# Last layer of a four-layer graph network: whole tiles for four of its elementwise steps, transposes in pairs of banks, and a fixed order on every engine

## The chip, the cores and the metric

One core of a Trainium2 chip. A core has five engines with queues of their own: TensorE (PE, with its weight loads shown apart as PEld), VectorE (DVE), ScalarE (ACT), GpSimd (POOL) and SyncE (SP, which here only issues DMAs). They share the on-chip memory SBUF; PE writes its results to PSUM, eight banks of 512 f32 columns in each of the 128 partitions. An engine works through its queue in order and stops at an instruction whose inputs are not there yet. The metric is the device time of one execution in microseconds.

## What is computed

`reference(x, adj, ...)` runs four graph layers over 4096 nodes with 64 features, each followed by a residual and a layer norm: a Chebyshev polynomial, a gated attention, a decayed neighbour sum, and a hyperbolic layer. Only the last one is touched by the change:

```python
deg = jnp.maximum(adj.sum(axis=1, keepdims=True), 1e-08)
w = adj / deg
log_ij = _logmap(x[:, None, :], x[None, :, :], c)     # for every pair of nodes
agg = jnp.einsum('ij,ijc->ic', w, log_ij)
transformed = agg @ weight + bias
return _expmap(origin, transformed, c)
```

`_logmap` needs, for each pair (i, j), one inner product, and from it a number: `arctanh(n) / n` of a norm. The kernel computes this factor for each pair, multiplies `adj` by it, and multiplies the result by the matrix of node vectors.

## The kernel before

**Tiles.** The 4096 x 4096 matrix is cut into 8 x 8 tiles of 512 x 512, held as 128 partitions x 4 blocks x 512 columns (2048 columns). The factor is symmetric, so only the 36 tiles on and above the diagonal are worked on: `tiles` (L1469) lists them by rows, 8 tiles in the first row (the diagonal one first), then 7, 6, ... 1; the groups come in the order `seq`. Of a diagonal tile only the upper part is computed: its first half has 512 columns in each of two blocks, its second half 256. The other 28 tiles are used twice: the tile of A itself (`own`, at_d) is multiplied by the factor, and the tile on the other side of the diagonal (`mirrored`, at_m) by the transposed factor.

**Halves.** The loop (L1719) counts half tiles: n = 2t + h, two blocks, 1024 columns each (512 for the second half of a diagonal tile). For each half the steps are, with engine and line:

1. `product` (PE, L1507): inner products into `v_ps`, two PSUM banks, two such buffers.
2. `square` (ACT, L1516): w = v squared. Then `opposite` (PE, L1526) adds a second product to `v_ps`.
3. `less_one` (DVE, L1534): w less one, with a floor.
4. Ln (ACT, L1731), then rt = Exp(0.5 Ln w), the root (ACT, L1732), and w = Exp(-0.5 Ln w), the reciprocal root (ACT, L1758).
5. rt = max(v, ..) + rt (DVE, L1756); after it `v_ps` is free for the product two halves later.
6. rt = Ln(rt), the last logarithm (ACT, L1767).
7. f = min(rt, ..) x w, the factor (DVE, L1741), and own x f (DVE, L1744), two halves behind step 4.
8. `turn` (PE, L1552): four transposes of 128 x 128 into one bank "post", four times for an off-diagonal tile; after each bank one product with `mirrored` (DVE, L1554). A diagonal tile has one bank (L1545) and one such product (L1547).
9. `gather` (PE, L1568, L1580): per block, the node vectors times the own product into the lower half of a row's bank `sums_ps`, and times the mirrored product of the tile before into the upper half. The first of the upper ones is a matmul that carries in the sum so far (L1576); at the end ACT copies the upper half out (L1587). At the end of a row the lower half is copied out as well (L1591).

**What else runs there.** `seam` is a list of steps of which one is taken in each half: at first the last steps of the layer before (`ends`, L1273: norms and preparation, L1286 to L1228), then, for each finished row, `finals` (L1644): `first` (16 matmuls L1660, three DVE steps, four L1670 on ACT), `second`, `third`, `fourth`, `fifth` (layer norm and store). `right(i)` (L1456) prepares the right side for a new row: 12 matmuls (L1461) into two "post" banks and two copies on ACT (L1464).

**Order.** The program is handed to a scheduler, which puts each engine's instructions into an order by their place in the program and by its own estimate of when their inputs are there. Only some PE instructions (product, opposite, gather) are tied to program order by `in_order` (L205). DMAs of tiles are issued on SP, three buffers each for own and mirrored.

**PSUM.** Eight banks: `ps_v3` 2 x 2, `ps_a3` 2 (row sums), `ps_p3` 2 ("post", shared by transposes, right sides and seam).

Of the kernel before, what the change touches and what calls it, by code (L numbers as in the profile page):

```python
# [62 lines left out]
def gnn4_kernel(  # L63
# [144 lines left out]
    def cols(b):  # L208
        return slice(b * P, (b + 1) * P)
# [1229 lines left out]
    with tc.tile_pool(name="o3", bufs=1) as op, tc.tile_pool(name="cols3", bufs=3) as cols_p, tc.tile_pool(  # L1439
        name="w3", bufs=4  # L1440
    ) as wp3, tc.tile_pool(name="el3", bufs=3) as el, tc.tile_pool(name="f3", bufs=2) as fp, tc.tile_pool(
        name="r3", bufs=2
    ) as rp, tc.tile_pool(name="ps_v3", bufs=2, space=PSUM) as ps_v, tc.tile_pool(
        name="ps_a3", bufs=2, space=PSUM
    ) as ps_a, tc.tile_pool(name="ps_p3", bufs=2, space=PSUM) as ps_p:
        HB = CB // 2

# [40 lines left out]
        def columns(n):  # L1488

            i, j = tiles[n // 2]  # L1490
            return slice(2 * P if i == j and n % 2 else 0, GW)

        rights, sums, fs = {}, {}, {}
        vs, ws, rts = {}, {}, {}
        NU = 2 * NT

        def product(n):

            if n >= NU:
                return  # L1500
            i, j = tiles[n // 2]
            vs[n] = ps_v.tile([P, HB, GW], F32, name="v_ps")
            cs = columns(n)
            for k in range(HB):
                jb = j * CB + (n % 2) * HB + k
                half = slice(jb % 2 * F, jb % 2 * F + F)
                in_order(nc.tensor.matmul(  # L1507
                    vs[n][:, k, cs], lhsT=tr_c[half, jb // 2, :], rhs=rights[i][0][half, cs], start=True, stop=True
                ))

        def square(n):
            if n >= NU:
                return
            ws[n] = wp3.tile([P, HB, GW], F32, name="w3")
            cs = columns(n)
            nc.scalar.activation(ws[n][:, :, cs], vs[n][:, :, cs], AF.Square)  # L1516

        def opposite(n):
            if n >= NU:
                return  # L1520
            i, j = tiles[n // 2]
            cs = columns(n)
            for k in range(HB):
                jb = j * CB + (n % 2) * HB + k
                half = slice(jb % 2 * F, jb % 2 * F + F)
                in_order(nc.tensor.matmul(  # L1526
                    vs[n][:, k, cs], lhsT=tr_o[half, jb // 2, :], rhs=rights[i][1][half, cs],
                    start=False, stop=True, skip_group_check=True,
                ))

        def less_one(n):
            if n < NU:
                w = ws[n][:, :, columns(n)]
                nc.vector.tensor_scalar(w, w, -SCALE * SCALE, V_FLOOR * (V_FLOOR + 2.0) * SCALE**2, ALU.add, ALU.max)  # L1534

        def turn(n):

            t, h = n
            i, j = tiles[t]
            work = []  # L1540
            if i == j:
                tp = ps_p.tile([P, GW], F32, name="post", tag="post")
                for k in range(HB):
                    for b in range(HB):
                        nc.tensor.transpose(tp[:, cols(HB * k + b)], fs[t][:, b, cols(HB + k)], ident)  # L1545
                to = own[t][:, HB:CB, 0 : HB * P]
                work.append(lambda: nc.vector.tensor_tensor(to, tp.rearrange("p (k i) -> p k i", k=HB), to, ALU.mult))  # L1547
                return work
            for b in (HB * h, HB * h + 1):
                tp = ps_p.tile([P, GW], F32, name="post", tag="post")  # L1550
                for k in range(CB):
                    nc.tensor.transpose(tp[:, cols(k)], fs[t][:, k, cols(b)], ident)  # L1552
                to = mirrored[t][:, b, :]
                work.append(lambda to=to, tp=tp: nc.vector.tensor_tensor(to, tp, to, ALU.mult))  # L1554
            return work

        def gather(t, h, tm):

            if t is not None:
                i, j = tiles[t]  # L1560
                if i == j and h == 0:
                    sums[i] = ps_a.tile([P, GW], F32, name="sums_ps")
                bank = sums[i]
            else:
                bank = sums[seq[-1]]
            for k in (HB * h, HB * h + 1):
                if t is not None:
                    in_order(nc.tensor.matmul(  # L1568
                        bank[0:F, :], lhsT=nat_c[:, j * CB + k, :], rhs=own[t][:, k, :],
                        start=(i == j and k == 0), stop=(j == seq[-1] and k == CB - 1), skip_group_check=True,  # L1570
                    ))
                if tm is not None:
                    above, below = tiles[tm]
                    if k == 0 and above != seq[0]:

                        in_order(nc.tensor.matmul(  # L1576
                            bank[F:P, :], lhsT=ident[:, F:P], rhs=tb[:, gcols(below)],
                            start=True, stop=False, skip_group_check=True,
                        ))
                    in_order(nc.tensor.matmul(  # L1580
# [3 lines left out]
            work = []  # L1584
            if tm is not None and h:
                to = tb[F:P, gcols(tiles[tm][1])]
                work.append(lambda: nc.scalar.copy(to, bank[F:P, :]))  # L1587
            if t is not None and h and tiles[t][1] == seq[-1]:
                g = tiles[t][0]
                copy = nc.vector.tensor_copy if g == seq[-1] else nc.scalar.copy  # L1590
                work.append(lambda: copy(tb[0:F, gcols(g)], bank[0:F, :]))  # L1591
                seam.extend(finals(g))
            return work
# [113 lines left out]
        turns, late_turns, gathers = {}, {}, {}  # L1707

        for t in range(3):
            load_own(t)  # L1710
            load_mirrored(t)
        rights[seq[0]] = right(seq[0])
        product(0)
        square(0)
        less_one(0)
        opposite(0)
        product(1)
        n = 0
        while n < NU + 2 or turns or gathers:  # L1719
            if n % 2:  # L1720
                load_own((n + 1) // 2)
                load_mirrored((n - 1) // 2)
            after = gather(*gathers.pop(n)) if n in gathers else []
            turned = [w for what in turns.pop(n, []) for w in turn(what)]
            if n < NU:
                if n % 2 == 0:
                    fs[n // 2] = fp.tile([P, CB, GW], F32, name="f3")
                w, cs = ws[n][:, :, columns(n)], columns(n)
                rts[n] = el.tile([P, HB, GW], F32, name="rt3")
                rt = rts[n][:, :, cs]  # L1730
                nc.scalar.activation(w, w, AF.Ln)  # L1731
                nc.scalar.activation(rt, w, AF.Exp, scale=0.5)  # L1732
                square(n + 1)
                opposite(n + 1)
            if n >= 2 and n - 2 < NU:
                m = n - 2
                t, h = divmod(m, 2)
                cm = columns(m)
                hs = slice(h * HB, (h + 1) * HB)
                f, at = fs[t][:, hs, cm], own[t][:, hs, cm]  # L1740
                nc.vector.scalar_tensor_tensor(  # L1741
                    f, rts.pop(m)[:, :, cm], T_MAX, ws.pop(m)[:, :, cm], ALU.min, ALU.mult
                )
                nc.vector.tensor_tensor(at, at, f, ALU.mult)  # L1744
                diagonal = tiles[t][0] == tiles[t][1]
                before = t - 1 if t and tiles[t - 1][0] != tiles[t - 1][1] else None
                gathers[n + 1] = (t, h, before)
                if diagonal and h == 0:
                    late_turns[n + 1] = (t, 0)
                if not diagonal and h == 1:  # L1750
                    turns.setdefault(n + 1, []).append((t, 0))
                    turns.setdefault(n + 2, []).append((t, 1))
            for work in turned:
                work()
            if n < NU:
                nc.vector.scalar_tensor_tensor(rt, vs[n][:, :, cs], (1.0 + V_FLOOR) * SCALE, rt, ALU.max, ALU.add)  # L1756
                product(n + 2)
                nc.scalar.activation(w, w, AF.Exp, scale=-0.5)  # L1758
            late = turn(late_turns.pop(n)) if n in late_turns else []
            for work in after:  # L1760
                work()
            less_one(n + 1)
            for work in late:
                work()
            if 0 < n <= NU:
                rt = rts[n - 1][:, :, columns(n - 1)]
                nc.scalar.activation(rt, rt, AF.Ln, scale=1.0 / SCALE)  # L1767
            if n == NU - 6:
                seam += [ahead_of_last(g) for g in seq[-2:]]
# [58 lines left out]
```

## Time and profile before

| | us |
|---|---|
| median of 3 runs (1407.41 to 1412.98) | 1408.8 |
| the profiled execution: time | 1410.98 |
| the profiled execution: span | 1409.2 |
| busy in the span: PE / DVE / ACT | 1308.8 / 1051.4 / 805.0 |
| first square of the last layer (ACT L1516) starts | 972.07 |
| last gather matmul (PE L1580) ends | about 1387.95 |

The trace has one entry for every instruction: start and duration, engine, line, what it writes and reads with its shape, and in brackets how long its engine sat idle before it and what that wait ended on. Durations of DVE and ACT instructions overlap their successors a little, so the distance from one start to the next is what an instruction costs a full engine. Matmul ends are modelled. The page divides the span into 40 slices of 35.2 us; the last layer is slices 28 to 40.

### The profile page before, as it was taken

What the parts mean: (1) busy time and instruction counts of PE and PEld (TensorE: products, weight loads), DVE (VectorE), ACT (ScalarE), POOL (GpSimd) and SP (SyncE); (2) the same over time, 40 slices, a digit from 0 to 9 for tenths busy, and PEclk for the clock granted to TensorE, in tenths of its full rate; (3) what the DMA queues carried; (4) which work ended last, traced back from release to release, by engine and by line L of the source; (5) the groups of instructions that cost most, each with busy time, mean ns of one, the idle gap of its engine ahead of it and who ended that gap; (6) DMA issues with size and microseconds to landing.
All of it is one profiled execution on the core that took longest, in us unless ns stands there. A gap on an engine that the chain in (4) does not pass through costs nothing.

```text
span 1409.2 us, 18984 instructions
## 1 busy us (share of the span) xinstructions
PE 1308.8 (93%) x6766; PEld 605.2 (43%) x6766; DVE 1051.4 (75%) x2010; ACT 805.0 (57%) x1341; POOL 109.9 (8%) x191
## 2 busy tenths in 40 slices
PE   7999999999899999999999999997888898999883
PEld 5655555565344334444444323333333333333331
DVE  6699998999334257787885224356999999999996
ACT  4554444343000115654424675745989999999893
POOL 2111111101122000010111000000000000000000
PEclk9999999999999999999999999998999999999997
DMA  9999999999699999999985755534235353445320
GB/s 316 404 395 391 402 411 410 410 403 392 231 380 372 389 415 372 422 358 338 329 306 185 229 178 165 181 120 180 99 141 211 147 214 150 183 162 200 141 106 12
DMA packets 108191, 382.16 MB, mean 271 GB/s; under 512 B 20276, under 2 KB 20280, under 8 KB 76472
## 3 DMA queue, kind: packets, MB, share of 16 engines
q1 hardware_dynamic: 87096, 296.17, 56.8%
q0 software_dynamic: 12736, 76.29, 13.2%
q10 hardware_dynamic: 8256, 8.39, 1.7%
q8 instruction: 56, 0.92, 0.3%
q14 instruction: 47, 0.39, 0.1%
HBM read 294.05 MB, written 85.20 MB: 269 GB/s over the span
## 4 chain that ended last, share of the span: by engine, by line
PE 61%; ACT 15%; DVE 15%; DMA 5%; issue 3%; ACTq 0%; DVEq 0%; SPq 0%
PE pass L566 7%; PE tp L657 6%; PE w_ps L566 5%; DMA raw<-in_adj_dram 4%; PE cnt_ps L1380 4%; PE a_last L1111 4%; PE a_ps L1111 4%; PE pass L559 4%; PE acc_ps L1340 4%; PE h_ps L559 3%; PE wide_last L1102 2%; PE p_ps L1102 2%; DVE rt L1756 2%; ACT w L1731 2%; ACT rt L1732 2%
## 5 line engine op out<-in xcount | busy, mean ns | idle before, releaser
L664 ACT COPY at<-tp 128x512 f32<-128x512 f32 x248 | 127.9, 599 | 119.1 <-issue 95.9
L1385 ACT ACTIVATE wt<-cnt_ps 128x512 uint16<-128x512 f32 x210 | 116.5, 596 | 65.4 <-PE cnt_ps L1380 63.3
L688 DVE TENSOR_REDUCE dpart<-raw 128x4 f32<-128x2048 f32 x64 | 145.5, 2275 | 5.4 <-DMA raw<-in_adj_dram 5.2
L1568 PE MATMUL sums_ps<-at_d,some 128*64 128x512 f32 x288 | 146.3, 629 | 2.7 <-DVE at_d L1547 1.7
L690 DVE TENSOR_REDUCE lows<-raw 128x1 f32<-128x2048 f32 x64 | 145.5, 2274 | 0.0
L657 PE MATMUL tp<-ident,raw 128*128 128x128 f32 x1024 | 131.5, 281 | 8.3 <-DMA raw<-in_adj_dram 7.3
L657 PEld LDWEIGHTS tp<-ident,raw 128*128 128x128 f32 x1024 | 115.1, 143 | 45.6 <-issue 36.5
L1580 PE MATMUL sums_ps<-at_m,some 128*64 128x512 f32 x224 | 108.6, 606 | 0.0
L1507 PE MATMUL v_ps<-rv,tr_a 64*128 64x512 f32 (+1 forms) x288 | 82.2, 649 | 21.2 <-DVE rt L1756 20.9
L566 PE MATMUL pass<-at,cheb_n 128*128 128x512 f32 x224 | 99.2, 601 | 2.4 <-DVE cheb_n L588 1.9
L566 PE MATMUL w_ps<-at,cheb_n 128*128 128x512 f32 x208 | 93.5, 593 | 0.0
L1756 DVE SCALAR_TENSOR_TENSOR rt<-v_ps,rt 128x1024 f32<-128x1024 f32 x72 | 83.3, 1157 | 5.2 <-ACT rt L1732 4.7
L1380 PE MATMUL cnt_ps<-m,follow 128*64 128x512 fp8e4 x480 | 81.7, 391 | 4.6 <-ACT wt L1385 2.1
L1744 DVE TENSOR_TENSOR at_d<-at_d,f 128x1024 f32<-128x1024 f32 x72 | 83.4, 1158 | 0.1
L1741 DVE SCALAR_TENSOR_TENSOR f<-rt,w 128x1024 f32<-128x1024 f32 x72 | 83.3, 1160 | 0.1
L1554 DVE TENSOR_TENSOR at_m<-post,at_m 128x512 f32<-128x512 f32 x112 | 75.1, 682 | 10.1 <-PE post L1552 9.9
L1767 ACT ACTIVATE rt<-rt 128x1024 f32<-128x1024 f32 x72 | 72.1, 1005 | 11.2 <-DVE rt L1756 10.7
L1387 DVE TENSOR_SCALAR wt<-cnt_ps 128x512 uint16<-128x512 f32 x46 | 31.8, 692 | 59.0 <-PE cnt_ps L1380 59.0
L1731 ACT ACTIVATE w<-w 128x1024 f32<-128x1024 f32 x72 | 72.0, 1000 | 4.8 <-DVE w L1534 4.8
L1552 PE MATMUL post<-ident,f 128*128 128x128 f32 x448 | 68.9, 284 | 4.8 <-DVE at_m L1554 4.5
L1758 ACT ACTIVATE w<-w 128x1024 f32<-128x1024 f32 x72 | 72.4, 1006 | 0.6
L1732 ACT ACTIVATE rt<-w 128x1024 f32<-128x1024 f32 x72 | 72.4, 1005 | 0.6
(404 smaller groups left out, 2271.7 us busy)
## 6 DMA issues: line engine op xcount, KB each, us to landing
at<-adj_t SPq DMA_DIRECT2D x119, 1024.0 KB, 7.7
raw<-in_adj_dram SPq DMA_DIRECT2D x64, 1024.0 KB, 13.4
adj_t<-at POOLq DMA_DIRECT2D x62, 1024.0 KB, 8.2
at_d<-adj_t SPq DMA_DIRECT2D x36, 1024.0 KB, 4.6
at_m<-adj_t SPq DMA_DIRECT2D x28, 1024.0 KB, 6.7
m<-mask_t SPq DMA_DIRECT2D x120, 128.0 KB, 2.9
m<-mask_t SPq DMA_DIRECT2D x60, 256.0 KB, 4.2
mask_t<-mask ACTq DMA_DIRECT2D x28, 256.0 KB, 7.4
```

Source lines behind the costliest of these rows:

```text
L566: in_order(nc.tensor.matmul(ps, lhsT=cheb_n[:, jb, k : k + 2, :], rhs=rhs, start=first, stop=last))
L657: in_order(nc.tensor.transpose(tp[:, cols(b)], raw[:, b, cols(k)], ident))
L664: nc.scalar.copy(at[:, k, :], tp)
L688: in_order(nc.vector.tensor_reduce(dpart[:, g, c, :], raw, AX.X, ALU.add))
L690: in_order(nc.vector.tensor_reduce(lows[:, n : n + 1], raw.rearrange("p b j -> p (b j)"), AX.X, ALU.min))
L1111: in_order(nc.tensor.matmul(ps[q * F : (q + 1) * F, :], lhsT=nat_a[:, c * CB + k, 0:F], rhs=of[q if signed else 0][:, k, :], start=(c == 0 ...
L1380: in_order(nc.tensor.matmul(cnt[a][r * HP : (r + 1) * HP, :], lhsT=follow, rhs=chunks[c][odd][2 * a + r][:, k, :], start=(h == 2 * NB - 1) ...
L1385: in_order(nc.scalar.activation(wt[odd][a], cnt[a], AF.Relu, scale=-128.0))
L1568: in_order(nc.tensor.matmul(bank[0:F, :], lhsT=nat_c[:, j * CB + k, :], rhs=own[t][:, k, :], start=(i == j and k == 0), stop=(j == seq[-1] ...
L1580: in_order(nc.tensor.matmul(bank[F:P, :], lhsT=nat_c[:, above * GB + k, :], rhs=mirrored[tm][:, k, :], start=(k == 0 and above == seq[0]), ...
L1732: nc.scalar.activation(rt, w, AF.Exp, scale=0.5)
L1756: nc.vector.scalar_tensor_tensor(rt, vs[n][:, :, cs], (1.0 + V_FLOOR) * SCALE, rt, ALU.max, ALU.add)
```

## The change

Steps 4 (the reciprocal root only), 6 and 7 work on a whole off-diagonal tile at once (2048 columns); diagonal tiles keep their halves, as do the other steps. The transposes go into one buffer of two banks (`ps_u3`), eight at a time, with one product of 1024 columns behind them. In `gather` the carry-in matmul comes first. The row sums and "post" have one bank each instead of two. Buffers of w are two whole tiles instead of four halves, of rt two whole tiles instead of three halves. Every instruction of steps 1 to 9 is tied to the one before it on its engine (`chained`), in the order in which the new loop writes them; the instructions of seam and of `right` are not. The new loop takes one tile per turn, with two seam steps. Its core:

```diff
-        name="w3", bufs=4
-    ) as wp3, tc.tile_pool(name="el3", bufs=3) as el, ...
+        name="w3", bufs=2
+    ) as wp3, tc.tile_pool(name="el3", bufs=2) as el, ...
-        name="ps_a3", bufs=2, space=PSUM
-    ) as ps_a, tc.tile_pool(name="ps_p3", bufs=2, space=PSUM) as ps_p:
+        name="ps_a3", bufs=1, space=PSUM
+    ) as ps_a, tc.tile_pool(name="ps_u3", bufs=1, space=PSUM) as ps_u, tc.tile_pool(
+        name="ps_p3", bufs=1, space=PSUM
+    ) as ps_p:
+        def chained(ins):
+            engine = ins.ins.engine
+            if engine in behind:
+                tc.add_manual_dep(
+                    ins.ins, behind[engine],
+                    mybir.DependencyInfo(mybir.DependencyClass.NoSync, mybir.DependencyReason.DATA),
+                    reason="chained",
+                )
+            behind[engine] = ins.ins.name
+            return ins
+        def parts_of(t):
+            return [part(t, 0), part(t, 1)] if on_diagonal(t) else [(slice(0, CB), slice(0, GW))]
...
+        def root(t, h):
...
+            chained(nc.scalar.activation(w, w, AF.Ln))
+            chained(nc.scalar.activation(rts[t][:, hs, cs], w, AF.Exp, scale=0.5))
+        def over_root(t):
+            for hs, cs in parts_of(t):
+                w = ws[t][:, hs, cs]
+                chained(nc.scalar.activation(w, w, AF.Exp, scale=-0.5))
+        def plus_root(t, h):
...
+            chained(nc.vector.scalar_tensor_tensor(
+                rt, vs.pop((t, h))[:, :, cs], (1.0 + V_FLOOR) * SCALE, rt, ALU.max, ALU.add
+            ))
+        def logs(t):
+            for hs, cs in parts_of(t):
+                rt = rts[t][:, hs, cs]
+                chained(nc.scalar.activation(rt, rt, AF.Ln, scale=1.0 / SCALE))
+        def factor(t):
...
+            for hs, cs in parts_of(t):
+                chained(nc.vector.scalar_tensor_tensor(
+                    f[:, hs, cs], rt[:, hs, cs], T_MAX, w[:, hs, cs], ALU.min, ALU.mult
+                ))
+        def own_products(t):
+            for hs, cs in parts_of(t):
+                at = own[t][:, hs, cs]
+                chained(nc.vector.tensor_tensor(at, at, fs[t][:, hs, cs], ALU.mult))
+        def turn(t, h):
+            if not 0 <= t < NT or (h and on_diagonal(t)):
+                return
+            tp = turned[t, h] = ps_u.tile([P, HB, GW], F32, name="tp")
...
+            for b in range(HB):
                 for k in range(CB):
+                    chained(nc.tensor.transpose(tp[:, b, cols(k)], fs[t][:, k, cols(h * HB + b)], ident))
+        def turned_products(t, h):
...
+                to = mirrored[t][:, h * HB : (h + 1) * HB, :]
+            chained(nc.vector.tensor_tensor(to, tp, to, ALU.mult))
+        def copies_out():
+            while to_copy:
+                copy, to, bank, *row = to_copy.pop(0)
+                chained(copy(to, bank))
+                if row:
+                    seam.extend(finals(row[0]))
-        for t in range(3):
+        for t in range(2):
             load_own(t)
             load_mirrored(t)
         rights[seq[0]] = right(seq[0])
-        n = 0
-        while n < NU + 2 or turns or gathers:
...
+        product(0, 0)
+        for t in range(-1, NT + 1):
+            plus_root(t, 1)
+            turn(t - 1, 0)
+            product(t + 1, 1)
+            square(t + 1, 0)
+            opposite(t + 1, 0)
+            copies_out()
+            less_one(t + 1, 0)
+            root(t + 1, 0)
+            own_products(t - 1)
+            seam_step()
+            gather(t - 1, 0)
+            square(t + 1, 1)
+            opposite(t + 1, 1)
+            plus_root(t + 1, 0)
+            product(t + 2, 0)
+            less_one(t + 1, 1)
+            logs(t)
+            root(t + 1, 1)
+            over_root(t + 1)
+            turned_products(t - 1, 0)
+            turn(t - 1, 1)
+            if t == NT - 3:
                 seam += [ahead_of_last(g) for g in seq[-2:]]
+            seam_step()
+            factor(t)
+            turned_products(t - 1, 1)
+            gather(t - 1, 1)
+            load_own(t + 2)
+            load_mirrored(t + 1)
+            if t + 4 < NT and tiles[t + 4][0] not in rights:
+                i = tiles[t + 4][0]
                 rights[i] = right(i)
+        copies_out()
```

## The prediction

> **What bounds the kernel now.** I began with the page's forty slices: from the 28th on (about 975 us) DVE and ACT both read 9, so the last layer is a stage of its own, and the diff touches nothing else. Then I asked for the busy time of each engine in stretches of it. Columns: stretch, length, busy us (instructions) of each engine, granted clock, DMA share, GB/s.
>
> ```profile
> 1033.00:1378.00 345.00, 309.49 (x1479) 129.80 (x1480) 326.31 (x513) 329.01 (x471) 9.38 (x12) 0.99 0.43 166
> 1120.88:1142.14 21.26, 19.75 (x92) 7.58 (x92) 20.98 (x26) 20.72 (x23) 0.00 (x0) 1.00 0.53 203
> ```
>
> Columns are PE, PE load, DVE, ACT, POOL. Over 345 us DVE idles 18.7 and ACT 16.0; DMA is at 43%. No single engine sets the end, two nearly full ones do, with PE at 90% behind them. The second row is two undisturbed tiles, 10.63 us each. Their DVE timeline:
>
> ```profile
> 1131.51 1.22 DVE L1741 SCALAR_TENSOR_TENSOR f<-rt,w 128x1024 f32<-128x1024 f32 x1
> 1132.64 0.68 DVE L1554 TENSOR_TENSOR at_m<-post,at_m 128x512 f32<-128x512 f32 x1
> 1133.24 1.22 DVE L1744 TENSOR_TENSOR at_d<-at_d,f 128x1024 f32<-128x1024 f32 x1
> ...
> 1139.57 0.69 DVE L1534 TENSOR_SCALAR w<-w 128x1024 f32<-128x1024 f32 x1
> 1140.40 0.69 DVE L1554 TENSOR_TENSOR at_m<-post,at_m 128x512 f32<-128x512 f32 x1
> ...
> 1142.14 1.22 DVE L1741 SCALAR_TENSOR_TENSOR f<-rt,w 128x1024 f32<-128x1024 f32 x1
> ```
>
> Read starts, not durations: an instruction of 1.22 is followed after 1.13, since its last 0.09 overlap the next; 512 columns take 0.60. Between 1139.57 and 1140.40 lie 0.83 instead of 0.60, the one idle place (0.23) of the tile. On ACT, starts again:
>
> ```profile
> 977.75 0.62 ACT L1731 ACTIVATE w<-w 128x512 f32<-128x512 f32 x1
> 978.27 1.04 ACT L1758 ACTIVATE w<-w 128x1024 f32<-128x1024 f32 x1
> ...
> 1080.77 1.04 ACT L1731 ACTIVATE w<-w 128x1024 f32<-128x1024 f32 x1
> 1081.71 1.00 ACT L1516 ACTIVATE w<-v_ps 128x1024 f32<-128x1024 f32 x1
> 1082.62 1.05 ACT L1732 ACTIVATE rt<-w 128x1024 f32<-128x1024 f32 x1
> ...
> 1104.40 1.06 ACT L1732 ACTIVATE rt<-w 128x1024 f32<-128x1024 f32 x1
> 1105.49 1.06 ACT L1758 ACTIVATE w<-w 128x1024 f32<-128x1024 f32 x1
> 1106.45 1.04 ACT L1731 ACTIVATE w<-w 128x1024 f32<-128x1024 f32 x1
> 1107.52 1.06 ACT L1732 ACTIVATE rt<-w 128x1024 f32<-128x1024 f32 x1
> ```
>
> 0.52 for 512 columns, 0.945 for 1024, 0.905 for a square; but 1.07 to 1.09 where the next one needs what this one has just written or read (1106.45 to 1107.52). PE:
>
> ```profile
> 1126.67 0.64 PE L1568 MATMUL sums_ps<-at_d,some 128*64 128x512 f32 x1
> 1126.68 0.64 PE L1576 MATMUL sums_ps<-tb,ident 128*64 128x512 f32 x1
> ...
> 1129.40 0.33 PE L1552 MATMUL post<-ident,f 128*128 128x128 f32 x1
> 1129.66 0.39 PE L1526 MATMUL v_ps<-ro,some 64*128 64x512 bf16 x2
> ```
>
> Gather matmuls into the two halves of the bank run side by side; a gather with the carry-in matmul (L1576) takes 2.73, one without 1.87 (1122.08 to 1123.94).
>
> **Part 1: fewer, wider instructions.** An off-diagonal tile has on DVE one factor, one own product and two turned products in place of 2 + 2 + 4, on ACT one reciprocal root and one logarithm in place of 2 + 2. Nothing of 2048 columns is in the trace, so I extend the pitches: DVE 1.13 + 2 x 0.53 = 2.20, ACT 0.945 + 2 x 0.425 = 1.795. One instruction less is worth 0.067 on DVE (1.13 - 2 x 0.533) and 0.095 on ACT. For a tile: DVE from 6 x 1.13 + 6 x 0.60 = 10.38 to 4 x 1.13 + 2 x 0.60 + 2 x 2.20 = 10.12; over 28 off-diagonal tiles DVE is relieved of 7.5 us, ACT of 5.3. The eight diagonal tiles keep halves: nothing. The bounds on this are 0 (two 1024s cost what a 2048 does) and 17.5 us for DVE (the whole fixed part of a duration, 1.22 - 2 x 0.533 = 0.155, 112 times), for ACT 0 and 11 (1.05 - 2 x 0.425 = 0.20, 56 times). I take what lies between two starts, because that is what a full engine pays.
>
> [...]
>
> **Part 2: what the pinned order makes of it.** A saving on two engines that wait for each other counts only through the loop that returns first. I walk one undisturbed iteration with these rows, a wait across engines at 0.04 (1081.71 + 1.00 = 1082.71, the DVE L1534 behind it starts at 1082.75). Zero is the start of less_one(t+1,0).
>
> ACT: Ln at 0.73 (less_one 0.69 + 0.04), Exp 1.80, square(t+1,1) 2.75, logs(t) 3.65, Ln 5.45, Exp 6.52, over_root 7.60, square(t+2,0) 9.39, its end 10.39, next less_one **10.43**. The 0.50 copy hides while ACT waits for less_one.
>
> DVE: own_products 0.60, plus_root(t+1,0) 2.89 (Exp ends 2.85), less_one 4.02, turned_products(t-1,0) 4.62, factor(t) 5.75 (logs end 5.53), turned_products(t-1,1) 7.95, plus_root(t+1,1) 9.08 to 10.21, then it waits 0.22 for the square. So DVE idles 0.31 of 10.43.
>
> PE: own ends 2.89; four gather matmuls 2.93 to 4.80 (L1576 is put first and needs no product, so it runs in the idle time ahead of this), opposite 5.13, product(t+2,0) 6.19, turn(t-1,1) 7.38. It is needed at 7.95: **slack 0.57**. The wait that the single two-bank buffer adds, turn(t-1,1) for the end of turned_products(t-1,0) at 5.84, is over before PE arrives at 6.19; behind it on PE stand gather(t-1,1) and the next turn, for whom nobody waits before 9.2. If that cover went, factor(t), 2.20 long, would still lie between. On the other side the next L1576 ends 12.6, own at 13.3: slack 0.7.
>
> So the loop is ACT plus one less_one, 10.43 against 10.63: -0.2 a tile, less than half of what DVE was relieved of.
>
> **Part 3: diagonals, finals, ends.** DVE: the iteration ahead of a diagonal is 0.60 + 2.20 + 1.13 + 0.34 + 1.13 + 2.20 + 1.13 + 0.60 = 9.33; the diagonal's own, on ACT, 10.10; the next 10.57 (two copies no longer fit the wait). The finals of a row and a new right side add, for ACT, 0.8 (four L1670), 1.26 (third), 0.96 (L1464 twice), for DVE 2.2 - 0.31 = 1.9 (fourth and fifth): S = 4.9, or 3.8 if the 0.36 that ACT waits in each iteration takes its share of the first three. A row of L tiles is 30.0 + (L - 3) x 10.43 + S. Before, from the starts of the diagonal's L1741 (980.91, 1074.60, 1151.73, 1218.70, 1273.55, 1373.75):
> - 7 tiles 77.1, after 75.5 to 76.6; 6 tiles 67.0, after 65.1 to 66.2; 5 tiles 54.9, after 54.7 to 55.8; the last 4 + 3 + 2 100.2, after 90.0 + 3 S = 101.4 to 104.7. Together **-2.5 to +4**.
> - The first row, which also holds the decay layer's last steps (14.5 us of DVE): first less_one 973.1, fill iteration 7.0, then 10.1, 10.4, 12.2, 14.6, 10.9, 11.4, 10.4, 9.3 and a right side 0.8, so factor of the second diagonal starts at 1076.0 where the first half now starts at 1074.6: **+1.5**.
> - Drain: last factor to last gather is 14.2 now (1373.75 to 1387.95) with waits for L1552's banks; by the pinned order 1.73 + 1.13 + 1.73 + 1.9 + 1.9 and two of the finals' steps, about 10: **-4**. One "post" bank in the closing steps: 0 to 2, I take **+1**.
> - PE work of the seam (L1660, L1461) beyond the slack: 0 to 11 (below), I take **+3**.
>
> Middle of -2.5 to +4 is +0.75; 0.75 + 1.5 - 4 + 1 + 3 = **+2**. Loads: own tiles are issued after iteration t for t+2, mirrored for t+1, over 10 us ahead of use against 4.6 and 6.7 us to landing; SP has nothing else queued. At nothing. The profiled execution took 1410.98 (span 1409.2), 2.2 above the median of the runs shown; the differences I set on the median: 1408.8 + 2 = **1411**, no change that counts.
>
> **Rivals.**
> *Slower through PE.* Pinning makes PE wait in line. Nothing chained covers the seam's PE work: "first" is 16 matmuls, 2.05 us, "right" 12, 1.31, with one bank, so that its second half waits for an ACT copy that may stand behind a 1.8 us activation. Above the 0.57 to 0.7 of slack each microsecond delays turn(t-1,1), and with it DVE and ACT: 1.4 for first, 1.31 + 0.9 + 0.5 - 0.65 = 2.0 for right, 3.4 a row, seven rows, +24: 1433. For it: PE is 90% busy. Against it: these instructions aren't chained and may be placed in gaps. From about 1 us a row beyond my +3 it counts as slower.
> *Faster.* The fixed order takes away idle time too: DVE idles 19.4 us from 985 to 1378; half of that and the 7.5 of work are -17: 1392. For it: the waits in rows 1 and 5 to 7, and the drain. Against it: my walk leaves 0.31 idle in each iteration, 11 us in all.
> *Merging saves nothing* (ACT's 2048 costs two 1024s): the loop is 10.62, 28 x 0.2 = 5.6 more: 1416, at the edge of the forecast.
>
> **Numbers.** A measurement of this kernel can tell about 0.5% (7 us) from no change. Forecast 1411 with 1402 to 1416, 0.42 for within 0.5%; slower through PE or merging without a gain 0.34; faster 0.24. The range leaves out a tenth on each side: 1395 to 1430.
>
> **What would show it.** Right: 2048-column DVE starts 2.20 apart, ACT 1.8; undisturbed iterations of 10.4; DVE waiting for the square (less_one) by about 0.2. Wrong: DVE turned products waiting for turn, PE gathers behind L1461 or L1660, iterations beyond 10.8 (slower); DVE without idle places at 10.1 to 10.2 (faster). If the wait across engines is 0.1 instead of 0.04, each iteration gets 0.12 longer and 4 us are gone.

## The result and the profile after

The changed kernel takes 1418.35 us (median of 10 runs, 1413.38 to 1421.61); the kernel before, measured beside it, 1408.79 (10 runs, 1407.27 to 1412.98). The ratio is 1.0065, interval 1.0052 to 1.0078: **slower by 9.6 us**, 0.65%. The forecast was 1411, no change. The profiled execution of after took 1421.16 us, 10.2 above that of before. Its page:

```profile
span 1419.4 us, 18822 instructions
...
PE 1301.0 (92%) x6766; PEld 607.8 (43%) x6766; DVE 1043.8 (74%) x1898; ACT 802.6 (57%) x1285; POOL 109.6 (8%) x191
```

DVE is relieved of 7.6 us of work (1051.4 before), almost what the widths were priced at (7.5), ACT only of 2.4 (805.0 before, 5.3 priced), and the span is 10.2 us longer. So the time went into waiting. The stretch of the prediction's first row, and one undisturbed tile (same columns as there):

```profile
1033.00:1378.00 345.00, 302.18 (x1469) 129.65 (x1469) 317.85 (x408) 325.30 (x415) 7.96 (x12) 0.98 0.43 166
1052.04:1062.38 10.34, 8.44 (x46) 3.57 (x44) 10.33 (x11) 8.91 (x9) 0.00 (x0) 1.00 0.53 205
```

The undisturbed tile takes 10.34 where it took 10.63: the middle did get faster. Its successor on DVE:

```profile
1062.38 2.28 DVE L1601 SCALAR_TENSOR_TENSOR f<-rt,w 128x2048 f32<-128x2048 f32 x1
1064.58 1.22 DVE L1634 TENSOR_TENSOR at_m<-tp,at_m 128x1024 f32<-128x1024 f32 x1
1065.71 1.21 DVE L1584 SCALAR_TENSOR_TENSOR rt<-v_ps,rt 128x1024 f32<-128x1024 f32 x1
1067.24 0.69 DVE L1557 TENSOR_SCALAR w<-w 128x1024 f32<-128x1024 f32 x1 [0.32 <-ACT w L1537]
1067.85 2.28 DVE L1610 TENSOR_TENSOR at_d<-at_d,f 128x2048 f32<-128x2048 f32 x1
```

An instruction of 2048 columns is followed after 2.20 (1062.38 to 1064.58), and DVE waits 0.32 for the square, as the walk had it. On ACT:

```profile
1060.41 1.90 ACT L1593 ACTIVATE rt<-rt 128x2048 f32<-128x2048 f32 x1
1062.22 1.05 ACT L1569 ACTIVATE w<-w 128x1024 f32<-128x1024 f32 x1
```

1.81 from start to start, against an estimate of 1.795. To see where the time came from, I cut the span at four marks that both kernels have: the end of the copies that close the layer before (DVE, L1409), the first and the last `plus_root` of 512 columns (one in each diagonal tile), and the end of the last gather matmul. "Before the layer" is work that no edit touches; it differs by up to 4.3 us between the executions profiled, so stretches tell more than spans.

| one profiled execution of each | median of its runs | before the layer | fill | rows | drain | closing |
|---|---|---|---|---|---|---|
| before | 1408.8 | 967.7 | 12.3 | 394.9 | 13.1 | 21.3 |
| after | 1418.4 | 967.1 | 14.2 | 396.9 | 16.6 | 24.7 |
| free_order | 1411.2 | 964.8 | 12.4 | 394.4 | 14.1 | 24.7 |
| halves | 1417.7 | 963.4 | 14.2 | 398.9 | 13.1 | 24.7 |
| three_finals | 1415.4 | 964.2 | 11.6 | 395.3 | 13.8 | 21.9 |
| seam_early | 1408.8 | 964.1 | 14.0 | 396.4 | 14.6 | 18.0 |
| late_seam | 1413.9 | 964.1 | 13.6 | 394.2 | 13.7 | 24.7 |
| warm_fill | 1418.3 | 966.1 | 15.2 | 395.6 | 13.7 | 24.7 |
| carry_back | 1423.2 | 964.5 | 14.1 | 403.1 | 15.1 | 24.7 |
| free_early | 1406.2 | 965.9 | 9.9 | 401.1 | 14.7 | 18.0 |
| free_early_halves | 1391.1 | 965.6 | 12.4 | 384.6 | 12.1 | 17.5 |

After against before: fill +1.9, rows +2.0, drain +3.6, closing +3.4. By these marks three of the four, and most of the time, lie at the ends of the layer. But each line of the table is one execution, and stretches that no edit touches differ too: warm_fill and late_seam are edited in their first two turns alone, and their rows take 395.6 and 394.2, their drain 13.7, where after takes 396.9 and 16.6. So the 2 us of the rows can't be told from chance, and the drain's are looked at below.

**Fill.** ACT in after:

```profile
976.17 0.58 ACT L1537 ACTIVATE w<-v_ps 128x512 f32<-128x512 f32 x1
979.91 0.63 ACT L1569 ACTIVATE w<-w 128x512 f32<-128x512 f32 x1 [3.16 <-DVE w L1557]
```

The square is done at 976.75, but `less_one` (L1557) comes on DVE only at 979.48: ahead of it stand norm steps of the layer before (L1294 to L1301, 976.05 to 979.48) and, pinned there, a `plus_root`. The norm steps in turn wait for PE:

```profile
976.05 0.69 DVE L1294 TENSOR_TENSOR nat_a<-post,tr_a 128x512 f32<-128x512 f32 x1 [1.97 <-PE post L1290]
...
979.48 0.39 DVE L1557 TENSOR_SCALAR w<-w 128x512 f32<-128x512 f32 x1
```

And PE has a slow clock here. Its first products in after, and below them the same in three_finals (an experiment below that leaves the order of the fill as it is), with the norm step that waits:

```profile
970.16 2.93 PE L1527 MATMUL v_ps<-rv,tr_a 64*128 64x512 f32 x8
```

```profile
966.49 1.56 PE L1527 MATMUL v_ps<-rv,tr_a 64*128 64x512 f32 x8
970.70 0.69 DVE L1294 TENSOR_TENSOR nat_a<-post,tr_a 128x512 f32<-128x512 f32 x1 [1.24 <-PE post L1290]
```

From 967.5 to 974 the granted clock of after reads 0.50; in three_finals it reads 1.00 from the start of the fill (964.2) to 973.8. Counted from that start, the norm step comes at 9.0 in after and at 6.5 in three_finals, and the fill takes 14.2 and 11.6. The two kernels in the free order below, free_order and free_early, have the same order in the fill as each other and differ in the same way: a clock of 0.51 (965.0 to 971.9) and a fill of 12.4, a clock of 1.00 (966 to 975) and a fill of 9.9. So a spell at half clock, which some executions have and others don't, costs 2.5 us of the fill, and at the same clock the pinned order costs about 1.7 more than the free one. Before has a shorter spell here (0.50 from 968.5 to 971.9).

**Drain.** PE in after:

```profile
1381.22 3.64 PE L1654 MATMUL sums_ps<-at_d,some 128*64 128x512 f32 x4 [1.88 <-DVE at_d L1610]
1384.80 1.97 PE L1624 MATMUL tp<-ident,f 128*128 128x128 f32 x8
```

Four gather matmuls take 3.64 us here and eight transposes 1.97, where shortly before eight transposes took 1.06: from 1382 to 1385 the granted clock reads 0.50. The next turned product on DVE (1386.81) waits 2.79 for them. At full clock they would have been done 2.7 sooner (3.64 - 1.87, 1.97 - 1.06), as an estimate. The trace of warm_fill, whose program is the same from the third turn on, shows it, with a clock of 1.00 throughout:

```profile
1379.94 1.90 PE L1654 MATMUL sums_ps<-at_d,some 128*64 128x512 f32 x4 [1.88 <-DVE at_d L1610]
1381.78 1.09 PE L1624 MATMUL tp<-ident,f 128*128 128x128 f32 x8
```

Its drain takes 13.7. So 2.9 of the 3.6 us by which the drain of after is longer than that of before are a spell at half clock in this execution, 0.7 are left, and the trace of before has such a dip too (0.58 from 1379 to 1382).

**Closing.** ACT in after, row copies and ends of layer norms:

```profile
1388.93 0.58 ACT L1787 COPY tb<-sums_ps 64x512 f32<-64x512 f32 x1 [6.33 <-PE sums_ps L1654]
...
1403.71 1.43 ACT L290 ACTIVATE o_sb<-v,ln_s,ln_r 128x64 f32<-128x64 f32 x4 [0.53 <-DVE ln_s L288]
...
1414.74 1.43 ACT L290 ACTIVATE o_sb<-v,ln_s,ln_r 128x64 f32<-128x64 f32 x4 [1.25 <-DVE ln_s L288]
```

In before:

```profile
1375.52 0.58 ACT L1591 COPY tb<-sums_ps 64x512 f32<-64x512 f32 x1
...
1392.61 1.43 ACT L290 ACTIVATE o_sb<-v,ln_s,ln_r 128x64 f32<-128x64 f32 x4 [2.40 <-DVE ln_s L288]
```

The second-last row is copied out at 1388.93; in before the copy was at 1375.52, 13.4 earlier. Of the last three layer norms, the first started at 1392.61 in before and starts at 1403.71 here. As the last gather itself ends 6.8 later (1394.76 against 1387.95), 6.6 of the 13.4 and 4.3 of the 11.1 remain when counted from there. Three rows' final steps are left for the time after the loop, and they need the same buffers: the second-last row's `v` (DVE, L1739) starts only at 1405.32, because there are two buffers and the row ahead reads its own until its layer norm (1403.71 + 1.43), and the one "post" bank makes the later of the two `first` left (PE, L1733) wait 1.19 at 1398.49.

### The profile page after: what moved, and what is told of

It is laid out like the page before. It is cut to its first block, busy times and chain, and to the rows that moved or that the text cites. A ratio compares the mean times of both kernels' runs of the same rounds, so it can differ in the third digit from the quotient of the medians.

```text
span 1419.4 us, 18822 instructions
## 1 busy us (share of the span) xinstructions
PE 1301.0 (92%) x6766; PEld 607.8 (43%) x6766; DVE 1043.8 (74%) x1898; ACT 802.6 (57%) x1285; POOL 109.6 (8%) x191
## 4 chain that ended last, share of the span: by engine, by line
PE 60%; ACT 15%; DVE 14%; DMA 6%; issue 4%; ACTq 0%; DVEq 0%; SPq 0%
PE pass L566 7%; PE w_ps L566 6%; PE tp L657 6%; DMA raw<-in_adj_dram 5%; PE cnt_ps L1380 4%; PE a_last L1111 4%; PE a_ps L1111 4%; PE pass L559 4%; PE acc_ps L1340 4%; ACT w L1569 3%; ACT rt L1570 2%; PE wide_last L1102 2%; PE p_ps L1102 2%; PE h_ps L559 2%; DVE rt L1584 2%
## 5 line engine op out<-in xcount | busy, mean ns | idle before, releaser
L657 PE MATMUL tp<-ident,raw 128*128 128x128 f32 x1024 | 131.8, 282 | 11.6 <-DMA raw<-in_adj_dram 10.5
L1659 PE MATMUL sums_ps<-at_m,some 128*64 128x512 f32 x224 | 112.6, 627 | 0.0
L1569 ACT ACTIVATE w<-w 128x1024 f32<-128x1024 f32 x72 | 72.3, 1005 | 20.7 <-DVE w L1557 20.6
L1601 DVE SCALAR_TENSOR_TENSOR f<-rt,w 128x2048 f32<-128x2048 f32 (+2 forms) x44 | 78.6, 1797 | 1.5 <-ACT rt L1593 1.5
L1610 DVE TENSOR_TENSOR at_d<-at_d,f 128x2048 f32<-128x2048 f32 (+2 forms) x44 | 78.4, 1795 | 0.0
L1654 PEld LDWEIGHTS sums_ps<-at_d,some 128*64 128x64 f32 x288 | 35.1, 142 | 94.5 <-issue 47.5
L1634 DVE TENSOR_TENSOR at_m<-tp,at_m 128x1024 f32<-128x1024 f32 x56 | 67.9, 1213 | 5.8 <-PE tp L1624 5.7
L1537 ACT ACTIVATE w<-v_ps 128x1024 f32<-128x1024 f32 x72 | 69.6, 966 | 2.5 <-PE v_ps L1527 1.5
L1624 PE MATMUL tp<-ident,f 128*128 128x128 f32 x448 | 61.9, 282 | 8.8 <-DVE at_m L1634 7.3
```

Source lines behind the costliest of these rows:

```text
L657: in_order(nc.tensor.transpose(tp[:, cols(b)], raw[:, b, cols(k)], ident))
L1569: chained(nc.scalar.activation(w, w, AF.Ln))
L1654: chained(nc.tensor.matmul(bank[0:F, :], lhsT=nat_c[:, j * CB + k, :], rhs=own[t][:, k, :], start=(i == j and k == 0), stop=(j == seq[-1] ...
L1659: chained(nc.tensor.matmul(bank[F:P, :], lhsT=nat_c[:, above * GB + k, :], rhs=mirrored[tm][:, k, :], start=(k == 0 and above == seq[0]), ...
```

## Experiments

My theory after the result was "ends": whole tiles deepen the pipeline, so the loop starts and ends with more work outside it. The main rival was "pinning": the order written by hand is worse than the scheduler's. Each ratio is against the kernel before, run on the same chip.

**free_order.** The new kernel without its chain; product, opposite and gather are tied among themselves as in before.

```diff
 def chained(ins):
-    engine = ins.ins.engine
-    if engine in behind:
-        tc.add_manual_dep(ins.ins, behind[engine], ...)
-    behind[engine] = ins.ins.name
     return ins
...
-                chained(nc.tensor.matmul(
+                in_order(nc.tensor.matmul(
```

> The changed kernel with its order set free again on DVE, ACT and for the transposes (products, opposites and gathers stay tied on PE, as before the change). Theory 'ends': of the 9.6 us that the change cost, some 7 lie after the last plus_root (drain and closing steps), some 2 in the fill, about 1 in the body; whole tiles and the bank split stay, so the loss stays: 1414 to 1422. Rival 'pinning': the fixed order makes the engines wait in line in each iteration; free order wins it back: 1410 or less.

Measured 1411.19, ratio 1.0019 (1.0000 to 1.0038). Giving up the pinned order alone wins back 7.2 of the 9.6 us. In the profiles the fill is 1.7 shorter, with a spell at half clock in both, and the rows 2.5; the drain (14.1, no spell) is no shorter than the pinned one without a spell (13.7), and the closing is the same (24.7). "Ends" as the only cause is refuted; as one part it stands.

**halves.** Pinned as in the change, but every tile in halves.

```diff
 def parts_of(t):
-    return [part(t, 0), part(t, 1)] if on_diagonal(t) else [(slice(0, CB), slice(0, GW))]
+    return [part(t, 0), part(t, 1)]
```

> The changed kernel with reciprocal root, last logarithm, factor and own products by halves again in every tile, all else as changed. Theory 'ends': merging is worth 0.2 in each off-diagonal iteration (10.43 to 10.62), 28 of them, less about 1 in the drain, where the first half of an own product lets the gather start sooner: 1421 to 1425. Rival 'pinning': the merge is lost in waits anyway: 1418, no change against the changed kernel.

Measured 1417.65, ratio 1.0063 (1.0040 to 1.0087), no different from after. In the pinned order the wide instructions are worth nothing net: an undisturbed tile takes 10.41 (1058.05 to 1068.46) in place of 10.34, the rows of the profile take 2 longer, and the drain (13.1) is 0.7 shorter than that of whole tiles without a spell (13.7).

**three_finals.** A third buffer for the final steps.

```diff
-        name="r3", bufs=2
+        name="r3", bufs=3
```

> The changed kernel with three buffers instead of two for the tiles of the finals (v among them). Theory 'ends': in the closing steps three groups' finals are under way at once, and the second last group's v (L1739, at 1405.32) waits for the store's L290 of the group before it (from 1403.71); with a third buffer the closing stretch of 24.6 us gets 2 to 3 shorter: 1415 to 1416.5. Rival 'pinning': no change, 1418.

Measured 1415.4, ratio 1.0041 (1.0025 to 1.0058): 3 us back, and the closing falls from 24.7 to 21.9. The wait at 1405.32 is a real cost. (The profiled execution was the fastest of its runs, 1408.66; it has no spell at half clock at the start of the fill or in the drain.)

**seam_early.** Two more final steps in each of the last three turns.

```diff
             copies_out()
+            for _ in range(2 if t >= NT - 2 else 0):
+                seam_step()
```

> The changed kernel with two more seam steps in each of the last three turns of the loop, so that the finals of finished rows don't pile up behind the loop. Theory 'ends': the closing stretch gets 2 to 3.5 shorter, 1414.5 to 1416.5, if the steps don't delay the last products on DVE. Rival 'pinning': no change, 1418.

Measured 1408.78, ratio 0.9997 (0.9977 to 1.0018): all 9.6 us are gone. The closing is 18.0, 6.7 shorter, and the layer's four stretches together are 9.3 shorter. Of these, 2.0 stand in the drain, where this execution has no spell at half clock; against a pinned drain without one (13.7) it is 0.8 longer. So the profiles show some 6 us for the early steps, and what makes the rest of the 9.6 is not shown. Ends of the last three layer norms:

```profile
1391.83 1.43 ACT L290 ACTIVATE o_sb<-v,ln_s,ln_r 128x64 f32<-128x64 f32 x4
...
1399.46 1.43 ACT L290 ACTIVATE o_sb<-v,ln_s,ln_r 128x64 f32<-128x64 f32 x4 [1.77 <-DVE ln_s L288]
...
1402.48 1.43 ACT L290 ACTIVATE o_sb<-v,ln_s,ln_r 128x64 f32<-128x64 f32 x4 [1.25 <-DVE ln_s L288]
```

The first of them is 11.9 us earlier than in after, 9 if the layer's own earlier start is taken off. It cost the rows nothing that shows (396.4 against 396.9), so there was room for these steps between the waits.

**before_early.** The same idea in the kernel before, as a control: is this gain open to it as well?

```diff
-            for _ in range(2 if n == 0 else 1):
+            for _ in range(2 if n == 0 or n >= NU - 4 else 1):
```

> Control: the kernel before the change, with one more seam step in each of its last half-tile turns. Theory 'the change piles the finals up': before the change the finals of finished rows were nearly done when the loop ended (closing stretch 21.3 us), so there is little to win: 1407 to 1409. Rival 'early seam steps are good for any version and say nothing of the change': closing stretch 18, like the changed kernel with early steps: 1405 to 1406.

Measured 1410.66, ratio 1.0017 (1.0006 to 1.0028): no gain. So what early steps win back belongs to the change.

**warm_fill.** Twelve transposes of a constant, twice in each of the first two turns, whose results nobody reads, to keep PE busy in the fill.

```diff
+        def keep_busy(t):
+            if t <= 0:
+                tp = ps_u.tile([P, HB, GW], F32, name="tp")
+                for k in range(12):
+                    chained(nc.tensor.transpose(tp[:, 0, cols(k % CB)], ident, ident))
...
+            keep_busy(t)
```

> The changed kernel with four times 12 transposes of the identity, whose results nobody reads, chained into PE's order in the first two turns (t = -1 and 0), where PE stood idle for 2.5 to 3.1 us at a time and its granted clock in the trace fell to 0.50. Theory 'the fill loses because PE runs at half clock after it idled': the clock stays above 0.9 there, products take 1.1 instead of 2.1 us, the fill from 14.2 to some 12 us: 1414 to 1416.5. Rival 'the fill waits for DVE's norm steps, whatever PE's clock': 1418 to 1420, unchanged or a little slower for the transposes in the queue.

Measured 1418.33, ratio 1.0073 (1.0053 to 1.0092). The granted clock from 973 to 982 rose from 0.69 to 1.00, and the fill got no shorter (15.2 against 14.2). But the transposes came too late for the spell that counts: from 966 to 972.7, at the start of the fill, the clock still reads 0.50. And the first twelve (1.53 us, at 973.43) stand on PE ahead of matmuls (L1290) that the norm steps wait for, so that a small gain may be hidden. So this run says only that the second spell of the fill costs nothing that shows; three_finals says what the first one costs (2.5). A kernel that keeps PE busy ahead of the fill was not run.

**late_seam.** In the first turn the first seam step goes to the end of the turn, so that both stand behind the tile's own chain.

```diff
-            seam_step()
+            if t >= 0:
+                seam_step()
...
             load_mirrored(t + 1)
+            if t < 0:
+                seam_step()
```

> The changed kernel with both seam steps of its first turn (t = -1) behind the first tile's chain, so that less_one and max-plus-root of the first tile go ahead of the decay layer's norm steps on DVE. Theory 'fill': the second logarithm of the first tile waits 3.2 us for its less_one, which stands behind norm steps; the fill gets 1.5 to 3 shorter: 1415.5 to 1417. Rival 'the norm steps are due anyway, the tiles of the first row wait for them': 1418.

Measured 1413.92, ratio 1.0036 (1.0023 to 1.0049; the ratio leaves out one run of 5748 us). That is 4.4 us back, more than I had expected; ACT's wait in the fill falls from 3.16 to 2.15, and the fill is 0.6 shorter. Rows and drain are each 3 shorter in this profile, and the drain has no spell at half clock. Order on DVE in the first turn is a cost; that all 4.4 come from it is not shown.

**carry_back.** The carry-in matmul stands behind the first own product again, as in before.

```diff
-                if h == 0 and above != seq[0]:
-                    chained(nc.tensor.matmul(bank[F:P, :], lhsT=ident[:, F:P], ...))
...
+                        if k == 0 and above != seq[0]:
+                            chained(nc.tensor.matmul(bank[F:P, :], lhsT=ident[:, F:P], ...))
```

> The changed kernel with the carry-in matmul back behind the first own product of a gather. Theory of the prediction's walk: PE's slack behind the own products is 0.57 us, the carry-in takes 0.86; 0.3 us more in each iteration that has one (21 of 36), 6 us: 1424, and DVE's turned products wait for the transposes. Rival 'PE has room that the walk doesn't count': 1418.

Measured 1423.22, ratio 1.0107 (1.0086 to 1.0128): 4.9 worse than after. DVE:

```profile
1208.29 0.17 DVE L282 RECIPROCAL ln_r<-ln_s 128x4 f32<-128x4 f32 x1
1209.99 1.22 DVE L1634 TENSOR_TENSOR at_m<-tp,at_m 128x1024 f32<-128x1024 f32 x1 [1.53 <-PE tp L1624]
```

The turned product waits for `turn`, as the slower rival had it: from 1033 to 1378 such waits sum to 9.2 us, against 2.9 in after. In the change itself the slack of 0.57 holds because the carry-in goes first.

**single_banks.** Two buffers of one bank for the turned factors, two products of 512 columns.

```diff
-        name="ps_u3", bufs=1, space=PSUM
+        name="ps_u3", bufs=2, space=PSUM
...
-            chained(nc.vector.tensor_tensor(to, tp, to, ALU.mult))
+            for b, tp in enumerate(tps):
+                to = mirrored[t][:, h * HB + b, :]
+                chained(nc.vector.tensor_tensor(to, tp, to, ALU.mult))
```

> The changed kernel with the transposes in single banks again (two buffers of one bank in place of one of two) and one DVE product of 512 columns behind each. DVE gets 0.13 more in an off-diagonal tile, against 0.31 that it idles there: nothing in the body; the drain 0.5 to 1 shorter, as the first product starts after four transposes: 1417 to 1418.5. If pairs of banks had been worth the 0.067 each that the prediction priced, and DVE were full: +3.8, 1422.

Measured 1420.75, ratio 1.0083 (1.0064 to 1.0101): 2.4 worse than after, but the two intervals overlap. Pairs of banks are worth some 2 us at most in this order, and that is not clear of the noise.

**free_early.** free_order and seam_early together.

> The free order (1411.2) together with the two more seam steps in the last turns. Theory 'ends': its closing stretch of 24.7 us becomes 18 to 20, all else stays: 1405 to 1407. Rival 'the steps only helped where the order was fixed': 1411.

Measured 1406.17, ratio 0.9979 (0.9966 to 0.9991): below before, by 0.2%. (The profiled execution was the slowest of its runs, 1411.34.)

**end_all.** All remedies for the end in the pinned order: seam_early, three_finals, and halves in the last two tiles.

```diff
-            return [...] if on_diagonal(t) else [...]
+            return [...] if on_diagonal(t) or t >= NT - 2 else [...]
```

> The changed kernel with all three edits for its end: two more seam steps in the last three turns, three buffers for the tiles of the finals, and the last two tiles by halves, so that their gathers start after half an own product. Theory 'ends': 1408.8 less 1 to 3 for the drain (from 14.6 to about 13 us after the last plus_root): 1405.5 to 1408. Rival: the early steps have already taken all there is: 1409.

Measured 1410.45, ratio 1.0011 (0.9996 to 1.0026): nothing beyond seam_early, and the same drain (14.6). Halves in the last two tiles don't shorten it.

**free_early_halves.** free_early with the edit of halves: no chain, early final steps, every tile in halves. What is left of the change is the new loop as program order, whole-tile buffers, pairs of banks and the carry-in put first.

> Free order, early seam steps (1406.2) and halves in every tile. Theory 'merging is worth nothing net, since what two instructions less save is given back by steps that start later': 1405 to 1407.5. Rival 'in a free order, with DVE and ACT full, the saved 0.067 and 0.095 a piece count': 5 to 7 slower, 1411 to 1413.

Measured 1391.09 (4 runs, 1389.21 to 1394.05), ratio 0.9871 (0.9850 to 0.9892): **17 us faster than before**, 15 faster than free_early, where I had expected 1405 to 1413. The gain is in the rows (401.1 to 384.6 in the profiles). Waits from 985 to 1370 (total, times, longest), free_early:

```profile
PE v_ps L1519 <- DVE rt L1576: 16.0, 17, 2.4
ACT w L1561 <- DVE w L1549: 15.7, 17, 2.3
...
DVE f L1593 <- ACT rt L1585: 10.6, 12, 2.8
```

and free_early_halves:

```profile
PE v_ps L1519 <- DVE rt L1576: 4.7, 4, 1.4
...
ACT w L1561 <- DVE w L1549: 2.2, 4, 1.3
```

The factor's wait for the logarithm (10.6) is below 0.5 there. The granted clock over the rows is 0.97 in free_early and 1.00 here; what part of the gain that makes is not separated. My reading of the waits: behind an instruction of 2.2 us on DVE or 1.8 on ACT stands the step that the other engine needs next, and the factor of a whole tile can't start on the half whose logarithm is ready. Over its 337 us from 1033 to 1370, DVE is busy 326.44 and ACT 325.89, 97% each; in before it was 95% over 345.

## Why the prediction was right in its range and wrong in its sum

By its own marks (the starts of the diagonal tiles' factor, L1601 in after: 989.54, 1083.37, 1161.71, 1228.20, 1284.46, 1382.20):

| term | predicted | measured |
|---|---|---|
| first row, to the second diagonal's factor | +1.5 | +8.8 (1083.37 - 1074.60) |
| rows | -2.5 to +4, seam +3; sum +3.75 | -0.3 (78.3 + 66.5 + 56.3 + 97.7 = 298.8, before 299.15) |
| drain, last factor to last gather | -4 (14.2 to 10) | -1.6 (12.6) |
| closing | +1 | +3.4 |
| sum | +2 | +10.2 |

- **Part 1, the prices, held between starts.** 2.20 and 1.81 there, DVE's busy time down by 7.6, next to the 7.5 from starts and far from the 17.5 that whole durations would have given. ACT's busy time went down by 2.4 where 5.3 were priced; why is not shown.
- **Part 2, the walk, held.** 10.34 and 10.37 against 10.43, with the wait for the square at its place. What the walk had wrong is the other side: it gave halves in the same order 10.62, and they take 10.41. So merging buys 0.07 us a tile in place of 0.2, and the rows show no gain that is clear of chance.
- **Part 3, first row: the step that failed.** The term is mis-sized, +1.5 for a measured +8.8. By the walk the fill iteration was 7.0, less than the 8.10 of before (974.55 to 982.65):

```profile
974.55 0.68 DVE L1534 TENSOR_SCALAR w<-w 128x1024 f32<-128x1024 f32 x1
...
982.65 0.69 DVE L1534 TENSOR_SCALAR w<-w 128x1024 f32<-128x1024 f32 x1
```

From `less_one` to `less_one` it took 10.36 (973.39 to 983.75), because norm steps that aren't chained, and a chained `plus_root`, stand ahead of the second half's `less_one`. In three_finals, without the spell at half clock, it takes 9.64 (968.77 to 978.41), so the spell is about 0.7 of it. The sixth and seventh turns took 12.80 and 13.22 where 10.9 and 12.2 were reckoned with the right side. In the sixth DVE waits 1.25 for transposes (1040.79) after another spell at half clock (0.50 from 1032.5 to 1039); in late_seam, without one there, it takes 11.47. In the seventh DVE waits 0.92 (1047.73) behind a copy of the right side on ACT (L1479). I had added the norms' DVE time to full iterations, but not their place in a pinned queue, and reckoned with no spell of the clock.
- **Drain: right but for the clock.** About 10 was reckoned from the last factor to the last gather. After takes 12.6; warm_fill and late_seam, with the same steps at full clock, take 9.7. The 2.8 us that the turned product waits for PE at half clock were not in the sum. First row and drain belong together, since a deeper pipeline moves time from one to the other: -2.5 predicted, +7.2 measured.
- **Closing: the mechanism was incomplete.** I counted one bank, and not that a row copied out 13.4 us later leaves three rows' final steps behind the loop, with two buffers. seam_early removes the pile, and with it the loss.
- **The rivals.** "Slower through PE" gave the sign but not the cause: the turned products' waits for PE from 1033 to 1378 are 2.9 us in all, and the rows lost nothing. Its slack was tight, as carry_back shows. "Merging saves nothing" is true of the total (halves), though not by its reason, since ACT's 2048 columns did save. "Faster" named idle time as the thing to win; free_early_halves wins it, but by undoing the pinning and the merging; that 1391 meets its 1392 is chance.

So the measured 1418.35 lies inside the range and outside the forecast's own 1402 to 1416: an undisturbed tile was worked out correctly, and the two ends of the layer were not. That the range holds is in part luck: the rows came out 4 us below their term, since the +3 for PE work of the seam didn't show, and this hides half of what the first row lost beyond its own.

**Not settled.** The losses don't add up one by one: free_order wins 7.2, seam_early 9.6, both together 12.2. The ends and the order overlap. Which part of free_early_halves earns its 17 us against before was not separated: early final steps alone gave before nothing, and pairs of banks some 2 at most in the pinned order; the new program order, the buffers and the carry-in were not tried one by one. Pinning halves with early final steps wasn't run. The runs of after fall into two groups (1413.4 and 1413.8, the rest 1417.8 to 1421.6), and so do those of three_finals (1408.7 to 1410.2, the rest 1414.5 to 1416.7). The traced execution of after, 1421.16, has spells at half clock at the start of the fill and in the drain, the one of three_finals, 1408.66, has neither, and the two are worth some 5 us; so they may be why, but one trace of each doesn't show it. Neither is shown what decides whether an execution has such a spell, or whether the pinned order has them more often; part of the 9.6 us may be theirs.

## What to carry to other kernels

When two engines feed each other as here, the little that a wider instruction saves (2 x 1.13 - 2.20 = 0.06 us on DVE, 2 x 0.945 - 1.81 = 0.08 on ACT) is to be set against the wait of the other engine's next step for all of it: in the free order whole tiles cost 15 us where the work that they save on DVE was priced at 7.5. Price the ends of a loop by the same walk as its middle, with the real queue of each engine: what is pinned, what is not, and what stands in front. After a change that deepens a pipeline, look at what is left to do behind the loop and with how many buffers; with that work moved into the last turns, the whole loss was gone. And before explaining a few us from two traces, compare traces whose program is the same at that place: here they differ by 2.5 us in the fill and 2.9 in the drain.

## What was unexpected of the hardware

PE's granted clock falls to 0.50 in spells (967.5 to 974 in after, 968.5 to 971.9 in before), and the same work can meet a spell in one execution and none in the next. In the drain of after PE works 1.06 of 3.76 us (1377.46 to 1381.22), the clock reads 0.50 from about 1380.5 to 1387, and four gather matmuls take 3.64. In warm_fill PE works the same 1.06 of 3.76 us (1376.18 to 1379.94), the clock stays at 1.00, and they take 1.90. So the same stretch of little work went with a spell in one trace and with none in the other; what decides it, these traces don't show. What a spell cost went with who waited for PE: 2.5 us at the start of the fill and 2.9 in the drain, where DVE waited for it (1.97 and 2.79), and nothing that shows in the later part of the fill, where transposes without a use brought the clock to 1.00 (973 to 982 in warm_fill, 0.69 in after) and the time stayed (1418.33 against 1418.35).
